# Tokens of the last feed-forward turned by VectorE and DMA instead of TensorE

## The chip, the core and the metric

The kernel runs on one core of a Trainium2 chip. A core has five engines that each work through their own queue in order: TensorE (PE in the profile, with weight loads shown apart as PEld), VectorE (DVE), ScalarE (ACT), GpSimd (POOL) and SyncE (SP, which here only issues DMAs). They wait for each other by semaphores. The metric is the device time of one execution in microseconds; the time before the change is the median of three runs.

## The reference

The input is x of 16 x 256 tokens by 256 features, float32, and the computation is a "macaron" block:

```
x = x + 0.5 * ffn(layernorm(x), w1, b1, w2, b2)
x = x + attention(layernorm(x), Wq, Wk, Wv, Wo)     # 16 heads of 16, rotary, causal
x = x + 0.5 * ffn(layernorm(x), w1, b1, w2, b2)

ffn(x) = gelu(x @ w1q.T + b1) @ w2q.T + b2          # w1q: 1024 x 256, w2q: 256 x 1024
w?q    = clip(round(w / mean(|w|)), -1, 1)          # ternary weights
```

The layernorm has no weights. Only the last of the three lines, the second feed-forward, is changed.

## The kernel before

The 4096 tokens lie in 8 blocks of 512 (NBLK = 8, TB = 512), each block as a tile xs[i] of 128 partitions by 4 token tiles by 256 features (BT = 4). `ffn(ln, after)` builds one feed-forward; ln = 0 is the first, ln = 2 the last. Its `step(u)` (line 378 on) handles u = 8 i + f: block i, chunk f of the 1024 hidden features (8 chunks of 128). A step does, in program order:

- `up(i, f)`: four matmuls (two halves of the 256 features, each with a "high" float32r part and a "rest") into a PSUM tile m of 128 x 512. ScalarE then computes gelu twice, once rounded (`h_high`) and once whole (`h_whole`), and `h_rest` = whole - high is subtracted by POOL for f = 1, 3, 5 and by VectorE for the others.
- what prepares the next blocks: statistics of block i + 2 (`stats` on VectorE, one token tile in each of f = 4 to 7, then `finish_stats`: var and rstd on POOL), the normalizing of block i + 1 into `xn` at f = 3 (`prepare`, VectorE), its transposes at f = 5 and 6 (`turn_in`: four 128 x 128 transposes on TensorE into the PSUM tile "mm", ScalarE copies them out as the high part of xnT, VectorE subtracts for the rest), and the bias b2 added to the whole of xs[i] by POOL at f = 6 (`add_bias`; at f = 1 in the last block).
- `down(i', f')` for the step two back (LATE = 2): eight matmuls, four token tiles times high and rest. After a block's last one VectorE adds half of the result to xs and `store` issues two DMAs of 256 KB on SP.

So TensorE's order is up(f), down(f - 2), up(f + 1), down(f - 1) and so on: the rest of chunk f is wanted two steps after its up projection. PSUM holds two m tiles; `h_high` and `h_rest` have five buffers, `h_whole` three, `xn` one, each part of xnT two.

The order within each engine is that of the program: vector, scalar, tensor, gpsimd and sync are wrapped so that every call keeps its place (`InOrder`, lines 164 to 176), and that is why nearly all instructions carry line 172 in the profile and are told apart by their tiles. The DMAs of `store` alone are issued through the plain queue, and the scheduler places them.

The two flat tiles that held the unquantized weights at the start (`flat1`, `flat2`, 128 x 2048) serve the attention later as work space; of flat2 it uses the first 1024 columns.

Of the kernel before, what the change touches and what calls it, by code (L numbers as in the profile page):

```python
# [8 lines left out]
FP = mybir.dt.float32  # L9
FR = mybir.dt.float32r  # L10
AF = mybir.ActivationFunctionType
# [4 lines left out]
P = 128  # L16
D = 256
KC = D // P
FF = 1024
NFC = FF // P  # L20
# [9 lines left out]
def kernel(  # L30
# [17 lines left out]
    BT = 4  # L48
    TB = BT * P
    NBLK = NT // TB  # L50
# [4 lines left out]
    fp = ctx.enter_context(tc.tile_pool(name="ffn", bufs=2))  # L55
# [19 lines left out]
    b1_sb = const.tile([P, NFC], FP, name="b1_sb")  # L75
    b2_sb = const.tile([P, D], FP, name="b2_sb")
    cos_sb = const.tile([P, 2, HD], FP, name="cos_sb")
    sin_sb = const.tile([P, 2, HD], FP, name="sin_sb")
    xs = [state.tile([P, BT, D], FP, name=f"x_{i}") for i in range(NBLK)]

    flat1, flat2 = (state.tile([P, 2 * FF], FP, name=f"w_{n}") for n in range(2))
# [19 lines left out]
    for k in range(KC):  # L101
        rows = slice(k * P, (k + 1) * P)
        nc.sync.dma_start(out=wv[:, k, :], in_=wqkvT[rows, 2 * D :])
        for at in range(0, 2 * D, 4 * HD):
            n, j, e = at // D, at // P % 2, at // (4 * HD) % 2
            nc.sync.dma_start(
                out=wqk[:, k, n, j, :, e, :],
                in_=wqkvT[rows, at : at + 4 * HD].rearrange("p (r d) -> p r d", d=HD),
            )
    for at in range(0, P, HD):  # L110
        r, n = at // 32, at // HD % 2
        nc.sync.dma_start(
            out=wo[at : at + HD, :, :],
            in_=woT.rearrange("(k n r d) f -> n r d k f", n=2, r=4, d=HD)[n, r],
# [19 lines left out]
        out=mask_k,  # L134
        in_=mask_k,
# [28 lines left out]
    class InOrder:  # L164
# [11 lines left out]
    tensor, vector, scalar, gpsimd, sync = (  # L176
        InOrder(engine) for engine in (nc.tensor, nc.vector, nc.scalar, nc.gpsimd, nc.sync)
    )
# [4 lines left out]
    def stats(ln, n):  # L183
        st = small.tile([P, 6], FP, name="st")
        vector.bn_stats(st, tokens(n))
        vector.bn_aggr(mv[ln][:, n, :], st)

    def finish_stats(ln, first, n):

        var = small.tile([P, BT], FP, name="var")  # L190
        gpsimd.tensor_scalar(
            var[:, 0:n], mv[ln][:, first : first + n, 1], LN_EPS, 1.0, ALU.add, ALU.mult
        )
        gpsimd.tensor_tensor(
            rstd[ln][:, first : first + n], var[:, 0:n], power[:, 0:n], ALU.pow
        )

    def normalize(ln, n, to, engine=None):
        (engine or vector).tensor_scalar(
            to,  # L200
            tokens(n),
            mv[ln][:, n, 0:1],
            rstd[ln][:, n : n + 1],
            ALU.subtract,
            ALU.mult,
        )
# [68 lines left out]

    LATE = 2

    def ffn(ln, after):
        xn, xnT, hT, ys = {}, {}, {}, {}

        def measure(i):
            if ln == 0:
                for t in range(BT):
                    stats(0, i * BT + t)
                finish_stats(0, i * BT, BT)

        def prepare(i, engine=None):
            xn[i] = fp.tile([P, BT, D], FP, name="xn", bufs=1)
            for t in range(BT):
                normalize(ln, i * BT + t, xn[i][:, t, :], engine)  # L290
            xnT[i] = [fp.tile([P, KC, TB], FR, name=f"xnT_{n}") for n in range(2)]

        def add_bias(i):
            gpsimd.tensor_add(xs[i], xs[i], b2_sb.unsqueeze(1).to_broadcast([P, BT, D]))

        def turn_in(i, k):
            tp = ps_mm.tile([P, TB], FP, name="mm")
            for t in range(BT):
                tensor.transpose(
                    tp[:, t * P : (t + 1) * P], xn[i][:, t, k * P : (k + 1) * P], ident  # L300
                )
            high, rest = (xnT[i][n][:, k, :] for n in range(2))
            scalar.copy(high, tp)
            return lambda: vector.tensor_sub(rest, tp, high.bitcast(FP))

        first = {}

        def up_first(i, f, to=None):
            h = first[i, f] = ps_m.tile([P, TB], FP, name="m") if to is None else to
            for n in range(2):  # L310
                for k in range(KC):
                    tensor.matmul(
                        h,
                        w1q[:, k, f * P : (f + 1) * P],
                        xnT[i][n][:, k, :],
                        start=(n == 0 and k == 0),
                        stop=(n == 1 and k == KC - 1),
                    )

        def up(i, f):  # L320
            if (i, f) not in first:
                up_first(i, f)
            h = first.pop((i, f))
            high = fp.tile([P, TB], FR, name="h_high", bufs=LATE + 3)
            rest = fp.tile([P, TB], FR, name="h_rest", bufs=LATE + 3)
            whole = fp.tile([P, TB], FP, name="h_whole", bufs=3)
            scalar.activation(high, h, AF.Gelu, bias=b1_sb[:, f : f + 1])
            scalar.activation(whole, h, AF.Gelu, bias=b1_sb[:, f : f + 1])

            engine = gpsimd if f in (1, 3, 5) and not (ln == 0 and i == NBLK - 1) else vector  # L330
            engine.tensor_sub(rest, whole, high.bitcast(FP))
            hT[i, f] = (high, rest)

        def down(i, f):
            if f == 0 and ln == 2 and i == NBLK - 1:

                ys[i] = [ps_mm.tile([P, 2, D], FP, name="mm") for t in range(0, BT, 2)]
            elif f == 0:
                y = ps_w.tile([P, BT, D], FP, name="w")
                ys[i] = [y[:, t : t + 2, :] for t in range(0, BT, 2)]  # L340
            parts = hT.pop((i, f))
            order = [(t, n) for t in range(BT) for n in range(2)]
            if ln == 2 and (i, f) == (NBLK - 1, NFC - 1):

                order = [(t, n) for n in range(2) for t in range(BT)]
            for t, n in order:

                tensor.matmul(
                    ys[i][t // 2][:, t % 2, :],
                    parts[n][:, t * P : (t + 1) * P],  # L350
                    w2q[:, f, :],
                    start=(f == 0 and n == 0 and t % 2 == 0),
                    stop=(f == NFC - 1 and n == 1 and t % 2 == 1),
                )
            if f == NFC - 1:
                for t in range(0, BT, 2):
                    xt = xs[i][:, t : t + 2, :]
                    vector.scalar_tensor_tensor(
                        xt, ys[i][t // 2], 0.5, xt, ALU.mult, ALU.add
                    )  # L360
                for t in range(0, BT, 2):
                    after(i, t)

        def begin():
            measure(0)
            if ln == 0:
                sizes(0)
            prepare(0)
            if ln == 0:
                threshold(0)  # L370
                signs(0, lambda w: w[:, :, 0 : FF // 2])
            for k in range(KC):
                turn_in(0, k)()
            if ln == 0:
                signs(0, lambda w: w[:, :, FF // 2 :])
                sizes(1)

        def step(u):
            i, f = divmod(u, NFC)
            if i < NBLK:  # L380
                up(i, f)
                if ln == 0 and u == 0:
                    threshold(1)
                if ln == 0 and u in (0, 3):
                    part = slice(0, NFC // 2) if u == 0 else slice(NFC // 2, NFC)
                    signs(1, lambda w: w[:, part, :])
                if ln == 0 and u == 4:
                    gpsimd.tensor_scalar(b2_sb, b2_sb, 0.5, 0.0, ALU.mult, ALU.add)
                if u == 1:
                    measure(1)  # L390
                if i + 1 < NBLK and (ln, i) != (2, 0):
                    if f == 3:
                        prepare(i + 1)
                    if f in (5, 6):
                        turn_in(i + 1, f - 5)()
                if f >= 4 and i + 2 < NBLK:
                    stats(ln, (i + 2) * BT + f - 4)
                    if f == NFC - 1:
                        finish_stats(ln, (i + 2) * BT, BT)
                if f == (1 if i == NBLK - 1 else 6):  # L400
                    add_bias(i)
            if u >= LATE:
                down(*divmod(u - LATE, NFC))
            if ln == 0 and u == 2 * NFC + 2:
                make_tables()
            if ln == 0 and u < (NBLK - 1) * NFC and later:
                later.pop(0)()

        return begin, step, prepare, turn_in, up_first
# [437 lines left out]
```

## Time and profile before

| What | Value |
|---|---|
| median of three runs | 602.25 us (601.55 to 603.68) |
| the profiled execution | 601.82 us, of which span 600.0 us |
| granted TensorE clock in it, mean | 0.998 |
| last feed-forward, from the first up projection of block 1 to that of block 2, and so on to block 7, by the chain | 16.03, 16.08, 16.10, 16.08, 16.10, 16.08 us |
| TensorE not busy in each of these | 0.02 us at most |
| VectorE, ScalarE, POOL busy in a block of 16.10 us | 10.55, 11.08, 7.87 us |
| DMA traffic in such a block | 34 GB/s, 0.10 of the engines' time |

The last feed-forward's steps run from about 466 us to the end. A profile line of a timeline gives the start, the duration, the engine, the line, the operation with its tiles (output <- inputs) and shapes, and in brackets how long the engine had been idle and what released it. A line of the chain gives start, duration, engine, tile and how many instructions were merged. Busy times of TensorE come from modelled ends of matmuls.

### The profile page before, as it was taken

The numbers are of one execution on the slowest core, as the hardware profiler recorded it, in microseconds if no ns is written. First come the engines' busy times: TensorE is split into PE (matmuls) and PEld (weight loads), VectorE is DVE, ScalarE is ACT, GpSimd is POOL, SyncE is SP. The second block draws the span as 40 slices with busy tenths as digits, with TensorE's granted clock in tenths as the row PEclk, the third lists the DMA queues.
The fourth block names the chain that finished last, engine by engine and source line by source line (L and its number), as shares of the span: only waits on it lengthen the run. The fifth ranks groups of instructions, "written<-read, shape, count | busy, mean of one in ns | idle before, by whom it ended". The sixth has DMA issues, their size and how long they took to land.

```text
span 600.0 us, 14402 instructions
## 1 busy us (share of the span) xinstructions
PE 581.9 (97%) x5388; PEld 467.1 (78%) x5388; DVE 475.3 (79%) x1695; ACT 391.2 (65%) x668; POOL 323.6 (54%) x297
## 2 busy tenths in 40 slices
PE   4999999999999999999999999999999999999996
PEld 3788999887777777777777777777767888888886
DVE  6877888677698998899999998888996466666643
ACT  4676766675476676676667666676665667666764
POOL 3645565693555576455765567454721354554442
PEclk9999999999999999999999999999999999999999
DMA  8810000000010001100111001100000011111101
GB/s 289 188 26 1 2 1 9 27 1 19 20 38 28 21 29 38 38 22 19 38 39 37 22 19 38 39 23 27 28 4 2 2 35 37 36 36 35 36 25 46
DMA packets 25588, 21.26 MB, mean 35 GB/s; under 512 B 11056, under 2 KB 21168, under 8 KB 25520
## 3 DMA queue, kind: packets, MB, share of 16 engines
q1 hardware_dynamic: 24960, 19.44, 10.2%
q8 instruction: 42, 0.69, 0.5%
q10 hardware_dynamic: 560, 0.92, 0.4%
q14 instruction: 26, 0.21, 0.1%
HBM read 7.51 MB, written 4.19 MB: 20 GB/s over the span
## 4 chain that ended last, share of the span: by engine, by line
PE 87%; DVE 6%; ACT 3%; issue 1%; DMA 1%; POOL 1%; DVEq 0%; SPq 0%; ACTq 0%; POOLq 0%
PE mm L172 34%; PE w L172 30%; PE m L172 23%; DVE masked L172 1%; DMA w<-in_w1T_dram 1%; DVE xn L172 1%; DVE w L172 1%; ACT h_high L172 1%; ACT h_whole L172 1%; DVE w2q L172 1%; DVE h_rest L172 1%; DVE st L172 0%; POOL h_rest L172 0%; DVE x L172 0%; ACT pT L172 0%
## 5 line engine op out<-in xcount | busy, mean ns | idle before, releaser
L172 DVE CUSTOM_DVE_ANT_0 masked<-m,mask_q 128x128 f32<-128x128 f32 x480 | 141.9, 351 | 22.2 <-PE m L172 20.9
L172 PE MATMUL m<-xnT,w1q 128*128 128x512 f32 x504 | 143.5, 406 | 0.8 <-ACT xnT L172 0.7
L172 ACT ACTIVATE pT<-w 128x768 f32<-128x768 f32 x128 | 104.1, 814 | 61.7 <-DVE w L172 61.3
L172 ACT ACTIVATE h_high<-m,b_sb 128x512 fp32r<-128x512 f32 x126 | 86.7, 688 | 79.2 <-PE m L172 79.1
L172 PE MATMUL w<-qT,kT 32*128 32x256 f32 (+1 forms) x1024 | 121.4, 348 | 1.5 <-ACT pT L172 1.5
L172 DVE TENSOR_TENSOR h_rest<-h_whole,h_high 128x512 fp32r<-128x512 f32 x83 | 74.6, 899 | 60.4 <-ACT h_whole L172 60.0
L172 PE MATMUL w<-w2q,h_high 128*128 128x256 f32 x480 | 120.7, 285 | 0.1
L172 PE MATMUL w<-w2q,h_rest 128*128 128x256 f32 x480 | 118.0, 279 | 0.7 <-POOL h_rest L172 0.7
L172 PEld LDWEIGHTS w<-qT,kT 32*128 32x128 f32 x1024 | 90.6, 184 | 35.3 <-issue 21.6
L172 PE MATMUL m<-kT,qT 32*128 32x128 f32 x960 | 116.8, 350 | 0.3 <-ACT kT L172 0.3
L172 POOL TENSOR_TENSOR h_rest<-h_whole,h_high 128x512 fp32r<-128x512 f32 x45 | 60.0, 1334 | 85.6 <-ACT h_whole L172 85.3
L172 PEld LDWEIGHTS m<-xnT,w1q 128*128 128x128 f32 x504 | 87.3, 191 | 16.3 <-DVE xnT L172 2.9
L172 PEld LDWEIGHTS w<-w2q,h_rest 128*128 128x128 f32 x480 | 90.4, 188 | 5.8 <-POOL h_rest L172 1.2
L172 PEld LDWEIGHTS w<-w2q,h_high 128*128 128x128 f32 x480 | 90.3, 188 | 5.0 <-DVE w2q L172 0.8
L172 DVE TENSOR_TENSOR w<-w,mask_k 128x512 f32<-128x512 f32 x128 | 88.9, 695 | 4.3 <-PE w L172 4.1
L172 ACT ACTIVATE h_whole<-m,b_sb 128x512 f32<-128x512 f32 x126 | 85.7, 680 | 0.0
L172 POOL TENSOR_TENSOR o<-avs,inv 128x256 f32<-128x256 f32 x32 | 20.3, 635 | 93.1 <-DVE inv L172 93.1
L172 PEld LDWEIGHTS m<-kT,qT 32*128 32x128 f32 x960 | 67.6, 185 | 2.3 <-DVE maxes L172 0.9
L172 PE MATMUL mm<-xnT_a,wqk 128*128 128x256 f32 x256 | 68.5, 392 | 0.0
L172 POOL TENSOR_TENSOR w<-w,cosT 128x512 f32<-128x512 f32 x32 | 41.2, 1288 | 26.8 <-ACT kT L172 13.5
L172 PEld LDWEIGHTS mm<-xnT_a,wqk 128*128 128x128 f32 x256 | 45.8, 189 | 10.0 <-issue 1.3
L172 POOL TENSOR_TENSOR w<-w,sinT 128x512 f32<-128x512 f32 x32 | 40.9, 1277 | 20.4 <-DMA w<-w 20.4
(86 smaller groups left out, 881.0 us busy)
## 6 DMA issues: line engine op xcount, KB each, us to landing
w<-w SPq DMA_DIRECT2D x64, 128.0 KB
out_dram<-x SPq DMA_DIRECT2D x15, 256.0 KB
x<-in_x_dram SPq DMA_DIRECT2D x7, 512.0 KB
w<-in_w2T_dram SPq DMA_DIRECT2D x1, 1024.0 KB
qT<-mT SPq DMA_DIRECT2D x64, 4.0 KB
w<-in_w1T_dram SPq DMA_DIRECT2D x1, 512.0 KB
w<-in_w1T_dram ACTq DMA_DIRECT2D x1, 512.0 KB
wqk<-in_wqkvT_dram SPq DMA_DIRECT2D x16, 32.0 KB
```

The source lines that it names most:

```text
L172: return tc.keep_in_program_order(getattr(self.engine, name)(*args, **kwargs))
```

## The change

In the last feed-forward, blocks 3 to 7 (`by_blocks`) are no longer transposed by TensorE. VectorE turns the whole normalized block in 32 x 32 pieces into the upper half of flat2 (`turned`). A DMA writes that to a DRAM tile (128 partitions of 4 KB), and four DMAs read it back in pieces of 512 bytes so that features lie on partitions, into the tile that later holds the rest part of xnT. `turn_in` then has ScalarE copy the high part from there, and VectorE subtracts in place.

The tokens come back in another order (a, n, t) than the matmuls of the down projection want, so both gelus of these blocks read and write through rearranged views with runs of 32.

For blocks 3 to 7 the work of preparing moves: statistics are taken two blocks ahead at f = 0 (one tile), 1 (one) and 2 (two), with var and rstd at f = 2; normalizing comes in two halves at f = 4 and 5 (for block 3 at f = 6 and 7), two blocks ahead; the transpose and the DMAs' issue at f = 7. In blocks 1 to 6 the bias is added in two halves at f = 2 and 3 instead of once at f = 6.

```diff
+    turned = flat2[:, FF:]
+    dram = ctx.enter_context(
+        tc.tile_pool(name="rows", bufs=2, space=bass.MemoryType.DRAM)
+    )
...
+        by_blocks = range(3, NBLK if ln == 2 else 0)
...
+        def normalize_by_blocks(i, t0, t1):
+            if t0 == 0:
+                xn[i] = fp.tile([P, BT, D], FP, name="xn", bufs=1)
+            for t in range(t0, t1):
+                normalize(ln, i * BT + t, xn[i][:, t, :])
+
+        def turn_by_blocks(i):
+            vector.transpose(turned, xn[i].rearrange("p n (j t) -> p j n t", t=32))
+            rows = dram.tile([P, 2 * TB], FP, name="rows")
+            sync.dma_start(out=rows, in_=turned)
+            of = rows.rearrange("(a f) (k j q) -> j f k a q", a=4, k=KC, j=4)
+            xnT[i] = [fp.tile([P, KC, TB], FR, name=f"xnT_{n}") for n in range(2)]
+            for j in range(4):
+                sync.dma_start(
+                    out=xnT[i][1][32 * j : 32 * j + 32]
+                    .bitcast(FP)
+                    .rearrange("p k (a q) -> p k a q", a=4),
+                    in_=of[j],
+                )
+
+        def add_bias(i, t0=0, t1=BT):
+            xt = xs[i][:, t0:t1, :]
+            gpsimd.tensor_add(xt, xt, b2_sb.unsqueeze(1).to_broadcast([P, t1 - t0, D]))
...
         def turn_in(i, k):
+            if i in by_blocks:
+                high, rest = (xnT[i][n][:, k, :] for n in range(2))
+                scalar.copy(high, rest.bitcast(FP))
+                return lambda: vector.tensor_sub(rest, rest.bitcast(FP), high.bitcast(FP))
...
-            scalar.activation(high, h, AF.Gelu, bias=b1_sb[:, f : f + 1])
-            scalar.activation(whole, h, AF.Gelu, bias=b1_sb[:, f : f + 1])
+            for to in (high, whole):
+                if i in by_blocks:
+                    to = to.rearrange("p (n a t) -> p a n t", n=BT, a=4)
+                    of = h.rearrange("p (a n t) -> p a n t", n=BT, a=4)
+                else:
+                    of = h
+                scalar.activation(to, of, AF.Gelu, bias=b1_sb[:, f : f + 1])
...
-                    if f == 3:
+                    if f == 3 and i + 1 not in by_blocks:
                         prepare(i + 1)
                     if f in (5, 6):
                         turn_in(i + 1, f - 5)()
-                if f >= 4 and i + 2 < NBLK:
-                    stats(ln, (i + 2) * BT + f - 4)
-                    if f == NFC - 1:
-                        finish_stats(ln, (i + 2) * BT, BT)
-                if f == (1 if i == NBLK - 1 else 6):
+                if i + 2 < NBLK:
+                    early = i + 2 in by_blocks
+                    for at in [(0,), (1,), (2, 3), (), (), (), (), ()][f] if early else (f - 4,):
+                        if at >= 0:
+                            stats(ln, (i + 2) * BT + at)
+                        if at == BT - 1:
+                            finish_stats(ln, (i + 2) * BT, BT)
+                    half = f - (6 if i + 2 == by_blocks.start else 4)
+                    if early and half in (0, 1):
+                        normalize_by_blocks(i + 2, 2 * half, 2 * half + 2)
+                    if early and f == 7:
+                        turn_by_blocks(i + 2)
+                if ln == 2 and 0 < i < NBLK - 1:
+                    if f in (2, 3):
+                        add_bias(i, 2 * (f - 2), 2 * (f - 1))
+                elif f == (1 if i == NBLK - 1 else 6):
                     add_bias(i)
```

More of the change, by code (lines that the diff above doesn't have):

```diff
@@ L291, in prepare @@
             xnT[i] = [fp.tile([P, KC, TB], FR, name=f"xnT_{n}") for n in range(2)]
-        def add_bias(i):
-            gpsimd.tensor_add(xs[i], xs[i], b2_sb.unsqueeze(1).to_broadcast([P, BT, D]))
+        def normalize_by_blocks(i, t0, t1):
[19 more added lines that the diff above has]
+            gpsimd.tensor_add(xt, xt, b2_sb.unsqueeze(1).to_broadcast([P, t1 - t0, D]))
         def turn_in(i, k):
+            if i in by_blocks:
+                high, rest = (xnT[i][n][:, k, :] for n in range(2))
+                scalar.copy(high, rest.bitcast(FP))
+                return lambda: vector.tensor_sub(rest, rest.bitcast(FP), high.bitcast(FP))
             tp = ps_mm.tile([P, TB], FP, name="mm")
```

## The prediction

> **What bounds the kernel now.** I read, in this order: the page's busy table and chain of waits, the chain in order of time for the last feed-forward, the timelines of GpSimd (POOL), VectorE (DVE), ScalarE (ACT) and SyncE (SP) there, and the granted clock and DMA traffic in short windows.
>
> ```profile
> span 600.0 us, 14402 instructions
> PE 581.9 (97%) x5388; PEld 467.1 (78%) x5388; DVE 475.3 (79%) x1695; ACT 391.2 (65%) x668; POOL 323.6 (54%) x297
> PE 87%; DVE 6%; ACT 3%; issue 1%; DMA 1%; POOL 1%; DVEq 0%; SPq 0%; ACTq 0%; POOLq 0%
> ```
>
> TensorE (PE) is 87% of the chain. In the part that the change touches it is all of it (chain in order of time: start, us, engine, tile):
>
> ```profile
> 508.32 0.44 PE mm L172 x4
> 508.76 0.94 PE w L172 x8
> 509.69 0.93 PE m L172 x4
> 510.62 0.44 PE mm L172 x4
> ...
> 513.87 0.69 PE m L172 x3
> 514.57 0.50 PE m L172
> ```
>
> Here "m" x4 is one up projection (0.93), "w" x8 one down projection (0.93), "mm" x4 one column half of the tokens being transposed (0.44). A step is 0.93 + 0.93 = 1.87 us and a block eight steps. Blocks start about 16.08 us apart: 8 x 1.87 = 14.9, two transposes 0.88, and about 0.26 at "514.57", where the fourth matmul of a block's first up projection is late: 0.69 + 0.50 = 1.19 instead of 0.93. The timeline shows why:
>
> ```profile
> 510.96 2.40 POOL L172 TENSOR_TENSOR x<-x,b_sb 128x1024 f32<-128x1024 f32 x1
> 511.96 1.95 DVE L172 TENSOR_TENSOR h_rest<-h_whole,h_high 128x512 fp32r<-128x512 f32 x1 [0.59 <-ACT h_whole L172]
> 513.83 0.68 DVE L172 TENSOR_TENSOR xnT<-mm,xnT 128x512 fp32r<-128x512 f32 x1
> ```
>
> The subtraction h_rest takes 0.69 elsewhere. Begun while POOL adds the bias, it ends 0.55 after POOL does (513.36 to 513.91), so the last xnT, which TensorE needs, is late. That is the first thing to carry into the change: on this chip POOL and a VectorE subtraction of two SBUF tiles exclude each other, while xnT, whose input is in PSUM, runs at 0.69 beside POOL (510.13, inside POOL's 509.70 to 510.99).
>
> The second is POOL's timing in a block:
>
> ```profile
> 485.13 1.03 POOL L172 TENSOR_TENSOR rstd<-var,power 128x4 f32<-128x4 f32 x1
> 516.28 0.19 POOL L172 TENSOR_SCALAR var<-mv 128x4 f32<-128x4 f32 x1 [2.92 <-DVE mv L172]
> 517.71 1.10 PE L172 MATMUL m<-xnT,w1q 128*128 128x512 f32 x4
> 519.59 1.09 PE L172 MATMUL m<-xnT,w1q 128*128 128x512 f32 x4
> 520.15 0.69 DVE L172 TENSOR_TENSOR h_rest<-h_whole,h_high 128x512 fp32r<-128x512 f32 x1 [0.88 <-ACT h_whole L172]
> 522.06 1.29 POOL L172 TENSOR_TENSOR h_rest<-h_whole,h_high 128x512 fp32r<-128x512 f32 x1 [2.44 <-ACT h_whole L172]
> 471.22 0.39 PE L172 MATMUL w<-w2q,h_rest 128*128 128x256 f32 x1 [0.34 <-POOL h_rest L172]
> ```
>
> The up projections of f = 2 and 3 start at 517.71 and 519.59; their rests can start 2.44 (DVE) and 2.47 (POOL) later. POOL sat idle 2.44 us before the rest of f = 3. The last line is an instance of TensorE waiting for a late POOL rest.
>
> **Removed.** Five blocks (3 to 7) lose two transposes each: 10 x 0.44 = 4.4 us off TensorE's chain. Nothing else can take that room, so it is gained whole unless a wait fills it.
>
> **Bias in halves at f = 2 and 3 (blocks 1 to 6).** The full addition leaves f = 6, so the last rests and xnT no longer meet it: six stalls of 0.26 = 1.6. VectorE now does the normalizing and the xnT subtraction from SBUF in that place, both of which can wait for POOL; I keep 1.4 as gained. Bounds: 0 to 1.6.
>
> **What stands on POOL's queue.** This is the step that I think decides. In the built kernel's order POOL runs in blocks 1 to 5: rest f = 1, var, rstd, first bias half, rest f = 3, second half, rest f = 5. Var waits for the statistics of the block two ahead, now done at f = 0, 1 and twice at f = 2 on VectorE, the last two behind the rest of f = 2. Times from the start of the up projection of f = 2:
> - VectorE's rest starts at 2.44; the next operation starts 0.61 later; two pairs of statistics take 0.55 + 0.64 (st 0.42, aggregate 0.18, gaps). Done at 4.24.
> - POOL: var starts 0.09 later, 4.33; rstd 0.27 after that, 4.60, and takes 1.03: 5.63.
> - First bias half, 128x512: the page's POOL products of that shape take 1288 ns: 6.92.
> - The rest of f = 4 on VectorE is ready at 2 x 1.87 + 2.44 = 6.18, held by the bias half, so it goes first when that ends: 0.55, to 7.47.
> - Rest of f = 3 on POOL, ready since 1.87 + 2.47 = 4.34: 7.47 + 1.30 = 8.77; if it goes before VectorE's, 8.22.
> - TensorE wants it for the second matmul of the down projection of f = 3, after up f = 5: 3 x 1.87 + 0.93 + 0.12 = 6.65.
>
> So TensorE waits 1.6 to 2.2 us per block, counting up to 0.1 from release to matmul. I take 2.15, the case in which VectorE's waiting rest goes first, as in the row at 513.36. In block 1 the transposes of block 2 still stand before that matmul (0.44 more cover): 1.8. Together 4 x 2.15 + 1.8 = 10.4; bounds 5 x 1.6 - 0.4 = 7.6 and 5 x 2.25 = 11.3. Block 6 has the halves but no statistics: its first half ends before the rest of f = 3 is ready, no cost. After the stall POOL runs the second half and rest f = 5, ending about 11.5; TensorE asks for that at 12.6, so it is covered by 1.1.
>
> **VectorE's transpose, 128x1024.** Rows: 128x256 from SBUF 437 ns, 128x512 from PSUM 717. Their slope gives 1.28, four times the first 1.75. It stands between the rest of f = 7 and that of f = 0, which it just reaches: 1.28 costs nothing, 1.75 up to 0.5 once or twice and later statistics. I take 0, range 0 to 2.5. Against it stands the Trainium skill, VectorE: DVE Perf Modes, "Rules for kernel authors": for a full 128x128 transpose use TensorE. By that rule alone the 4.4 would not be a gain; the chain rows decide that it is.
>
> **DMAs.** SP's built order is: rows to DRAM, two stores of the block before, four reads. The reads stand behind stores that wait for the down projection of f = 7. Counted from a block's start: the transpose ends near 2.5, the rows' DMA needs about 2.9 (a pair of 256 KB stores issued at 518.70 had moved its data by 521.3, at 340 GB/s, and some 0.3 for completion); the stores go out at about 5.0 and 5.7, the reads (0.4 to 0.55 each to issue) from 6.0 to 8.0. Store traffic ends near 7.6; 512 KB of reads at 340 GB/s end near 9.5, at a third of that rate near 12.5. ScalarE copies from them at 11.7 at the earliest and, with the stall above, may do so until 14.5. (The stores' issue, and two of the short windows, whose last three columns are granted clock, DMA share and GB/s:)
>
> ```profile
> 518.70 0.97 SPq L743 DMA_DIRECT2D out_dram<-x  x2
> 520.10:520.50 0.40, 0.40 (x3) 0.33 (x2) 0.35 (x1) 0.01 (x1) 0.00 (x0) 1.00 1.04 353
> 598.25:598.50 0.25, 0.00 (x0) 0.00 (x0) 0.00 (x0) 0.00 (x0) 0.00 (x0) 0.50 0.99 332
> ```
>
> So I charge 0. Bounds 0 and, at the 50 GB/s that 64-byte pieces got near 24 us, 10 us of reading, some 3.3 late per block: 15. The pieces here are 512 bytes, nearer to the loads' 1 KB at 350 GB/s. The stores, queued behind the rows' wait for the transpose, have no reader; the last block's, which end the kernel, have no rows before them.
>
> **Gelu writing in pieces of 32.** The vals copy writes pieces of 16 at 372 ns, as long as the contiguous mT copy: 0, upper bound 0.04 each, 0.4 in all. The xnT subtraction now reads SBUF twice and waits for POOL's rest of f = 5; it ends near 12.0 and 13.9 after the base above, TensorE wants the second at 14.1, so no cost. The Trainium skill, SBUF — State Buffer, "Who interferes with whom", says that a VectorE instruction with two SBUF inputs contends with POOL's reads. If each waited a whole POOL rest and this were on the path, an estimate by that page would add 5 x 1.3.
>
> **Sum.** -4.4 - 1.4 + 10.4 = +4.6. The profiled run took 601.82 (span 600.0, 1.82 around it): 606.4. The median of the runs shown is 602.25, 0.43 above it: 606.9. Ends of the main case: -6.0 + 7.6 = +1.6 and -4.4 - 0.5 + 11.3 = +6.4, plus transposes +2.5: 603.9 to 611.
>
> **Rivals.**
> - POOL in time: the wait at down f = 3 isn't there, and the gains stand: 602.25 - 5.8 = 596.4. It needs var, rstd and the half to end by 5.3 instead of 6.92; below a stall of 1.16 per block (5.8 / 5) the change is faster. For it: POOL is busy only 54%. Against: it is a queue in order, and each duration is a row. 0.11.
> - Reads late: they land after 14.5, that is at less than some 75 GB/s. Then ScalarE, with gelu queued behind the copy, holds the block's first up projection: up to 602.25 + 4.6 + 15 = 622. 0.06.
> - VectorE the bound: a slower transpose and normalizing held by POOL make it late at two more places; 1 us in each of 5 blocks: 612. Or TensorE's clock falls in the stalls: it was still 1.00 until 598.0, 2.5 us after the last matmul (near 595.5), and 0.50 from 598.25; stalls of over 2.6 might halve it. 0.06.
> - Main 0.75; gain and loss cancel, 0.02.
>
> **Range and chances.** 603.2 to 611.5 holds the main case and part of the third rival. Faster by over 0.3% (about what a measurement of this kernel can tell from none) 0.11, within it 0.04, slower 0.85.
>
> **What would show it.** Right: down f = 3 with an idle of about 2 us released by POOL's h_rest, five times; var about 2 us before it; no "mm" transposes in blocks 3 to 7; blocks 2 to 5 about 17.1 us apart, the last ones 15.0. Wrong: POOL's rest of f = 3 ending within 0.8 of its old place, or TensorE waiting for the xnT copy, that is for DMA.

## The result and the profile after

The changed kernel takes 607.93 us (median of six runs, 606.12 to 608.31) against 602.45 us for the kernel before (now the median of six runs, 601.55 to 603.68): a ratio of 1.0084, 95% interval 1.0072 to 1.0095, so it is slower by 5.5 us. The forecast was 606.9. The profiled execution has a span of 605.2 us, 5.2 more than before.

The page after, its span, busy times and the chain's shares by engine:

```profile
span 605.2 us, 14447 instructions
PE 577.6 (95%) x5348; PEld 463.8 (77%) x5348; DVE 489.8 (81%) x1700; ACT 391.4 (65%) x668; POOL 324.8 (54%) x303
PE 77%; DVE 8%; POOL 5%; ACT 4%; issue 3%; DMA 2%; SPq 0%; DVEq 0%; POOLq 0%; ACTq 0%
```

TensorE has 40 matmuls and 4.3 us of busy time less, as it should have without ten transposes of four matmuls each. But its share of the chain has fallen from 87% to 77%, and POOL and VectorE have come in. The chain in order of time shows one of the places, in block 3 (start, us, engine, tile; st holds statistics):

```profile
521.20 0.95 PE m L172 x4
522.17 0.69 ACT h_high L172
522.86 0.58 ACT h_whole L172
...
523.53 0.69 DVE h_rest L172
524.23 0.35 DVE st L172
...
525.40 0.19 POOL var L172
...
525.68 0.11 POOL rstd L172
525.79 0.88 issue
526.67 1.29 POOL x L172
527.96 1.69 POOL h_rest L172
529.65 0.04 issue
529.70 1.09 PE w L172 x7
```

The up projection of f = 2, its gelu, VectorE's rest of f = 2, the statistics behind it, then on POOL var, rstd ("issue" is the rest of its 1.02 us), the first half of the bias, the rest of f = 3, and only then TensorE's down projection. That is the queue that the forecast had written out. The list of waits from 480 us on gives it its size. "A <- B" says that A waited for B, and the columns are total us, times, the longest:

```profile
PEld w L172 <- POOL h_rest L172: 10.3, 5, 2.2
PE w L172 <- POOL h_rest L172: 8.8, 5, 1.9
```

These are five waits, one in each of blocks 1 to 5, seen once at the weight load and once at the matmul. No other wait of TensorE's in that stretch is over 0.3 us. The timelines of POOL, VectorE and TensorE at the same place show each step (start, us, engine, operation; in brackets idle before and releaser):

```profile
525.68 1.02 POOL L172 TENSOR_TENSOR rstd<-var,power 128x4 f32<-128x4 f32 x1
526.67 1.29 POOL L172 TENSOR_TENSOR x<-x,b_sb 128x512 f32<-128x512 f32 x1
527.91 1.73 POOL L172 TENSOR_TENSOR h_rest<-h_whole,h_high 128x512 fp32r<-128x512 f32 x1
...
527.20 1.32 DVE L172 TENSOR_TENSOR h_rest<-h_whole,h_high 128x512 fp32r<-128x512 f32 x1 [1.89 <-ACT h_whole L172]
...
527.57 0.28 PE L172 MATMUL w<-w2q,h_high 128*128 128x256 f32 x1
529.70 0.39 PE L172 MATMUL w<-w2q,h_rest 128*128 128x256 f32 x1 [1.85 <-POOL h_rest L172]
```

VectorE's rest of f = 4 is held by the bias half (1.32 instead of 0.69), then holds POOL's rest of f = 3 (1.73 instead of 1.30). TensorE's second matmul of the down projection would have followed at 527.69, 0.12 after the first, and comes at 529.70, 2.0 us late.

By the chain the blocks 1 to 6 are now 17.73, 17.04, 17.07, 17.05, 17.05 and 14.94 us apart; they were 16.03 to 16.10. Here are the first up projections of blocks 2 and 3, and of blocks 6 and 7:

```profile
500.42 0.93 PE m L172 x4
...
517.46 0.93 PE m L172 x4
...
568.63 0.93 PE m L172 x4
...
583.57 0.93 PE m L172 x4
```

The last feed-forward is taken from the start of ScalarE's load of the gelu table to that of VectorE's last addition. These lines bound it, two of the kernel before and two of the changed one:

```profile
466.09 1.28 ACT L172 ACT_TABLE_LOAD   x1
595.41 1.29 DVE L172 SCALAR_TENSOR_TENSOR x<-mm,x 128x512 f32<-128x512 f32 x2 [0.66 <-PE mm L172]
...
467.02 1.28 ACT L172 ACT_TABLE_LOAD   x1
600.48 1.29 DVE L172 SCALAR_TENSOR_TENSOR x<-mm,x 128x512 f32<-128x512 f32 x2 [0.67 <-PE mm L172]
```

It was 595.41 - 466.09 = 129.32 and is 600.48 - 467.02 = 133.46: 4.14 longer. Of the rest of the 5.2 in the span, 0.93 us lies ahead of it, among instructions that are the same in both programs, and 0.1 behind it. In the nine profiled executions of this study that table load starts anywhere from 465.98 to 467.88, while the table load before it starts within 165.85 to 166.40, so most of this difference arises between the two. Why is not settled here, so the experiments are read by both measures.

The clock bears on the 5.5 between the medians as well. Four of the six runs of the changed kernel had a mean granted TensorE clock of 0.996 or 0.997, and took 607.90 to 608.31 us. The other two had 0.998 and 0.999, and took 606.12 and 606.99; the slower of these is the profiled one. In the 63 runs of the experiments' rounds, which include runs of the kernel before, the mean was never under 0.998. In the nine traces the clock is under 1.00 only after the last matmul, which leaves a mean of 0.998 or more. So in those four runs the clock seems to have fallen at another place too. Where, and whether TensorE's waits brought it about, is not shown, as none of these four left a trace. The other two runs alone are 4.1 slower than the kernel before (606.55 - 602.45), as much as the feed-forward is longer.

### The profile page after: what moved, and what is told of

Its sections match the earlier page's. It is cut to its first block, busy times and chain, and to the rows that moved or that the text cites. A ratio compares the mean times of both kernels' runs of the same rounds, so it can differ in the third digit from the quotient of the medians.

```text
span 605.2 us, 14447 instructions
## 1 busy us (share of the span) xinstructions
PE 577.6 (95%) x5348; PEld 463.8 (77%) x5348; DVE 489.8 (81%) x1700; ACT 391.4 (65%) x668; POOL 324.8 (54%) x303
## 4 chain that ended last, share of the span: by engine, by line
PE 77%; DVE 8%; POOL 5%; ACT 4%; issue 3%; DMA 2%; SPq 0%; DVEq 0%; POOLq 0%; ACTq 0%
PE mm L172 30%; PE w L172 26%; PE m L172 20%; POOL h_rest L172 2%; POOL w L172 1%; DVE masked L172 1%; ACT h_high L172 1%; DVE h_rest L172 1%; ACT h_whole L172 1%; POOL x L172 1%; DMA w<-w 1%; DVE st L172 1%; DMA w<-in_w1T_dram 1%; DVE w L172 1%; DVE xn L172 1%
## 5 line engine op out<-in xcount | busy, mean ns | idle before, releaser
L172 PE MATMUL m<-xnT,w1q 128*128 128x512 f32 x504 | 141.6, 404 | 0.7 <-ACT xnT L172 0.7
L172 DVE TENSOR_TENSOR h_rest<-h_whole,h_high 128x512 fp32r<-128x512 f32 x83 | 71.3, 859 | 59.7 <-ACT h_whole L172 59.2
L172 POOL TENSOR_TENSOR h_rest<-h_whole,h_high 128x512 fp32r<-128x512 f32 x45 | 62.3, 1385 | 90.9 <-ACT h_whole L172 90.7
```

Source lines behind the costliest of these rows:

```text
L172: return tc.keep_in_program_order(getattr(self.engine, name)(*args, **kwargs))
```

## The experiments

The theory was that POOL's queue decides: the rest of f = 3 stands behind var, which waits for statistics, and behind rstd and a bias half. Its rivals were that VectorE and POOL exclude each other whatever the order, that VectorE is too full, that the split bias alone is at fault, and that tokens come late from DRAM.

| Kernel | Median us | Last feed-forward us | Against 129.32 |
|---|---|---|---|
| changed kernel | 607.93 | 133.46 | +4.14 |
| var and rstd behind the rest of f = 3 | 598.18 | 125.11 | -4.21 |
| rest of f = 3 on VectorE | 601.78 | 128.46 | -0.86 |
| bias whole at f = 6 | 607.45 | 133.80 | +4.48 |
| early statistics | 597.33 | 124.07 | -5.25 |
| bias halves alone | 601.07 | 127.63 | -1.69 |
| early statistics, reads ahead of stores | 597.65 | 123.38 | -5.94 |
| early statistics, turned a step later | 599.38 | 125.10 | -4.22 |

**Var and rstd behind the rest of f = 3.**

```diff
-                        if at == BT - 1:
+                        if at == BT - 1 and not early:
                             finish_stats(ln, (i + 2) * BT, BT)
+                    if early and f == 3:
+                        finish_stats(ln, (i + 2) * BT, BT)
```

> One move against the changed kernel: in blocks 1 to 5 var and rstd are issued behind POOL's rest of f = 3 instead of ahead of it. Queue theory (the rest of f = 3 is late because it stands behind work that waits for statistics): TensorE's wait at the down projection of f = 3, 2.0 us five times, goes; rstd now comes some 4 us later, so VectorE normalizes later and the xnT subtraction costs about 0.7 at the first up projection of blocks 3 to 6. Worked out: 602.45 - 4.4 - 1.4 + 4 x 0.7 = 599.4, range 597 to 601. Rival, exclusion of VectorE and POOL (they hold each other up whatever the order on POOL): the same work collides, 606 or more. Rival, TensorE waits for the tokens from DRAM: no change, 608.

Measured: 598.18 us, ratio to before 0.9923 (0.9907 to 0.9938). Two small instructions, moved behind the two larger ones that follow them in POOL's queue, turn a loss of 5.5 us into a gain of 4. From block 1 on, TensorE's waits no longer name POOL, and the wait that is left is for xnT. The chain shows the new order, and VectorE's line how long normalizing takes there:

```profile
PE m L172 <- DVE xnT L172: 0.8, 4, 0.2
PEld m L172 <- DVE xnT L172: 2.5, 4, 0.6
...
505.62 1.29 POOL h_rest L172
...
506.99 0.19 POOL var L172
...
507.27 1.03 POOL rstd L172
...
508.32 0.77 DVE xn L172
...
508.32 2.69 DVE L172 TENSOR_SCALAR xn<-x,mv,rstd 128x256 f32<-128x256 f32 x2 [0.19 <-POOL rstd L172]
```

What is left is the other wait that I expected here, xnT at the first up projections. Normalizing now starts behind the later rstd and runs while POOL is busy (2.69 us for two), so the xnT behind it is late. Blocks are 15.39 us apart there, 0.45 over 14.94, and I had taken 0.7. Exclusion as such, and the DRAM trip, fall as causes of the loss: both are still in this kernel. So does the half by itself, which still stands ahead of the rest of f = 3; what delays it is the pair that waits for statistics.

**The rest of f = 3 on VectorE.**

```diff
-            engine = gpsimd if f in (1, 3, 5) and not (ln == 0 and i == NBLK - 1) else vector
+            on_pool = (1, 5) if ln == 2 and i + 2 in by_blocks else (1, 3, 5)
+            engine = gpsimd if f in on_pool and not (ln == 0 and i == NBLK - 1) else vector
```

> In blocks 1 to 5 the rest of f = 3 is subtracted by VectorE instead of POOL, all else as in the changed kernel. Queue theory: the wait at the down projection of f = 3 goes, but POOL's rest of f = 5 still stands behind rstd and both bias halves and VectorE has 0.69 more: about 0.7 at the down projection of f = 5 and 0.9 at the next first up projection, in four blocks. 602.45 - 5.8 + 4 x 1.6 = 603, range 600 to 605. Rival, VectorE is the engine that is too full (489.8 us busy): one more subtraction on it makes it slower than 608.

Measured: 601.78 us, ratio 0.9991 (0.9980 to 1.0002). TensorE's waits of some size:

```profile
PE m L172 <- DVE xnT L172: 3.2, 4, 0.8
PEld w L172 <- POOL h_rest L172: 1.0, 4, 0.3
```

The big wait goes although VectorE has one subtraction more per block, so VectorE's fullness is not the cause. The new waits cost 1.28 us a block (blocks 16.22 apart) where I expected 1.6, and eat most of the gain.

**The bias left whole at f = 6.**

```diff
-                if ln == 2 and 0 < i < NBLK - 1:
-                    if f in (2, 3):
-                        add_bias(i, 2 * (f - 2), 2 * (f - 1))
-                elif f == (1 if i == NBLK - 1 else 6):
+                if f == (1 if i == NBLK - 1 else 6):
                     add_bias(i)
```

> The tokens turned as in the changed kernel, but the bias left whole at f = 6 as before. Queue theory: without the first half ahead of it the rest of f = 3 starts after rstd, 5.6 us after the up projection of f = 2, and ends 0.3 to 0.4 late, so that wait shrinks from 2.0 to 0.4; the whole bias of 2.4 us then meets the normalizing and xnT, which now read SBUF twice, and costs about 1.9 at the first up projection of blocks 3 to 7. 602.45 - 4.4 + 5 x 0.4 + 4 x 1.9 = 607.6, range 604 to 610: slow as before, but with the wait in another place. Rival, only the split bias is at fault: 598.

Measured: 607.45 us, ratio 1.0079 (1.0062 to 1.0097). The same loss, in another place:

```profile
PE m L172 <- DVE xnT L172: 7.2, 5, 1.5
PEld w L172 <- POOL h_rest L172: 2.0, 4, 0.7
```

Without the half in front, the rest of f = 3 is late by little; but the whole addition of 2.4 us now holds VectorE's normalizing and xnT. So the bias had to move once the tokens are turned from SBUF; it was moved into a place that was also taken.

**Early statistics.** Statistics two each at f = 0 and 1, var and rstd at f = 2, bias halves at f = 1 and 3, normalizing at f = 5 and 6.

```diff
-                    for at in [(0,), (1,), (2, 3), (), (), (), (), ()][f] if early else (f - 4,):
+                    for at in [(0, 1), (2, 3), (), (), (), (), (), ()][f] if early else (f - 4,):
...
-                        if at == BT - 1:
+                        if at == BT - 1 and not early:
                             finish_stats(ln, (i + 2) * BT, BT)
-                    half = f - (6 if i + 2 == by_blocks.start else 4)
+                    if early and f == 2:
+                        finish_stats(ln, (i + 2) * BT, BT)
+                    half = f - (6 if i + 2 == by_blocks.start else 5)
...
-                    if f in (2, 3):
-                        add_bias(i, 2 * (f - 2), 2 * (f - 1))
+                    if f in (1, 3):
+                        add_bias(i, f - 1, f + 1)
```

> All of the change kept, its pieces placed so that POOL never has a rest behind something that waits: statistics two each at f = 0 and 1, var and rstd at f = 2, bias halves at f = 1 and 3, normalizing at f = 5 and 6. Queue theory: POOL is through with rstd by the time that the rest of f = 3 is ready; nothing is left at the down projection of f = 3 and at most 0.1 at the first up projections: 602.45 - 4.4 - 1.4 = 596.7, range 595.8 to 598.5, faster than both kernels. Rival, exclusion of VectorE and POOL: as much work of both in the same block, 604 or more. Rival, reads from DRAM barely in time: they are asked for 2 us earlier against the block's work when the wait is gone, so TensorE waits for the xnT copy instead, 600 or more.

Measured: 597.33 us, ratio 0.9908 (0.9886 to 0.9930): faster than both kernels. From block 1 on, TensorE has no wait for POOL left. One wait of some size and of another kind shows, in one block, in ScalarE's and SP's timelines (its reads, and those of the round after it for comparison):

```profile
535.66 3.67 SPq L172 DMA_DIRECT2D xnT<-rows  x4
...
541.94 0.62 ACT L172 CAST xnT<-xnT 128x512 fp32r<-128x512 f32 x1 [1.26 <-DMA xnT<-rows]
...
551.33 2.54 SPq L172 DMA_DIRECT2D xnT<-rows  x4
```

ScalarE waits 1.26 us for the reads, and block 5's first up projection is 0.7 late. The feed-forward is 5.25 shorter; all of the ten transposes (10 x 0.44 = 4.4) and the six small stalls (6 x 0.26 = 1.56) would be 5.96.

**The bias halves alone.**

```diff
-        by_blocks = range(3, NBLK if ln == 2 else 0)
+        by_blocks = range(NBLK, NBLK)
```

> The bias halves of the change alone: TensorE transposes all blocks as before, statistics, normalizing and var/rstd at their old places. Theory: the six stalls of 0.26 at the first up projections go, since nothing of POOL's meets the last rests there; in block 1 the second half may hold VectorE's normalizing at f = 3. 602.4 - 1.6 + 0.5 = 601.3, range 600.6 to 602. Rival, the halves themselves delay POOL's rest of f = 3: 603 or more. Rival, the 0.26 comes from something else: 602.4.

Measured: 601.07 us against 602.78 in the same rounds, ratio 0.9970 (0.9958 to 0.9982). The six stalls of 0.26 are gone: no block's first up projection shows a late fourth matmul, block 2's for instance reads

```profile
498.77 0.93 PE m L172 x4
```

The feed-forward is 1.69 shorter, and the 0.5 that I added for block 1 doesn't appear. So the 0.26 was POOL's bias holding VectorE, and this half of the change gains by itself: POOL's queue has nothing waiting in it at f = 2.

**Reads ahead of stores.** On top of the early statistics, the stores' DMAs keep their program order.

```diff
-        parts = [(t, 2, nc.sync)]
+        parts = [(t, 2, sync)]
         if (i, t) == (NBLK - 1, BT - 2):
-            parts = [(t, 1, nc.sync), (t + 1, 1, nc.scalar)]
+            parts = [(t, 1, sync), (t + 1, 1, scalar)]
```

> The version with early statistics, and the stores of the output kept in program order, so that the four reads from DRAM are issued on SP as soon as the rows have landed and not behind a store that waits for the down projection. In that version ScalarE waited 1.26 us for the reads of one block and 0.36 in another, and TensorE lost 0.7 there. Theory: reads go out about 0.9 us sooner and no 256 KB store runs beside them; those waits go: 597.3 - 0.7 = 596.6, range 595.8 to 597.5. Rival, the reads' own traffic is slow in that block and not their start: the wait stays, 597.3.

Measured: 597.65 us, ratio 0.9910 (0.9897 to 0.9924); by medians it is not told apart from the version before it. In its one profile the wait is gone, and the feed-forward is 0.69 shorter, 5.94 in all, which is the whole of 5.96:

```profile
534.98 3.17 SPq L172 DMA_DIRECT2D xnT<-rows  x4
...
540.97 0.62 ACT L172 CAST xnT<-xnT 128x512 fp32r<-128x512 f32 x1
```

**Turned a step later.** On top of the early statistics, the transpose and its DMAs go from f = 7 to f = 0 of the next block.

```diff
+                if f == 0 and i + 1 in by_blocks:
+                    turn_by_blocks(i + 1)
...
-                    if early and f == 7:
-                        turn_by_blocks(i + 2)
```

> The version with early statistics, and VectorE's transpose with its DMAs issued one step later (f = 0 of the next block instead of f = 7), to measure how much cover the trip through DRAM has. In that version the first copy of a block waited 0 to 1.26 us for the reads. Theory: the rows land 1.9 us later and with them the reads 1.3 to 1.9, of which TensorE absorbs about 0.5: 5 blocks x 0.8 to 1.4 = 4 to 7, so 602.5, range 599.5 to 605, with TensorE waiting for xnT at the first up projections. Rival, the trip has 2 us and more of cover in most blocks, as I worked out beforehand: 597 to 598.5.

Measured: 599.38 us, ratio 0.9938 (0.9921 to 0.9954), feed-forward 1.0 longer than with early statistics: a miss between the two stated cases. In the first round the reads were issued only 0.7 later (rows at 503.53, reads at 506.70; with early statistics alone 502.23 and 506.00), and ScalarE waits for them in all five rounds, of which three:

```profile
511.76 0.62 ACT L172 CAST xnT<-xnT 128x512 fp32r<-128x512 f32 x1 [0.80 <-DMA xnT<-rows]
...
526.99 0.62 ACT L172 CAST xnT<-xnT 128x512 fp32r<-128x512 f32 x1 [0.84 <-DMA xnT<-rows]
...
542.89 0.62 ACT L172 CAST xnT<-xnT 128x512 fp32r<-128x512 f32 x1 [1.51 <-DMA xnT<-rows]
```

4.4 us of waiting on ScalarE cost TensorE 1.7, taken against the version in which ScalarE never waits for reads (125.10 - 123.38): some 0.5 of each wait is absorbed. So with POOL's wait gone the DRAM trip, begun a step later, has no cover to spare at ScalarE, and about half a microsecond more at TensorE. I had carried the whole delay of 1.3 to 1.9 over to ScalarE and most of it to TensorE; both were too much.

## Why the prediction was right

- **What POOL's queue would cost.** Counted from the up projection of f = 2 (521.04 in the timeline), forecast and measured: VectorE's rest starts 2.44 and 2.49; var 4.33 and 4.36; rstd 4.60 and 4.64; first half 5.63 and 5.63; its end 6.92 and 6.92; VectorE's rest of f = 4 ends 7.47 and 7.48; rest of f = 3 ends 8.77 and 8.60. The order "VectorE's waiting rest goes first" was the one that occurred. Only the last step is off by more than 0.05: POOL's rest took 1.73 from 527.91 on, partly beside VectorE's, where I had counted 1.30 after it. A block's wait is 17.05 - 14.94 = 2.11 for the 2.15 taken, block 1's 17.73 - 16.03 = 1.7 for 1.8: 10.1 in all (4 x 2.11 + 1.7) for 10.4. The experiments with var and rstd moved, and with the rest moved to VectorE, show that it is the place in this queue.
- **Transposes, 4.4.** Right, and whole: with the waits out of the way the feed-forward is 5.94 shorter, 4.4 of it from here.
- **The small stalls, 1.4.** They were worth all of 1.56; the halves alone gave 1.69.
- **Transpose on VectorE, 0.** It took 1.24 (1.28 by the slope) and cost nothing; its line is below. The Trainium skill (VectorE: DVE Perf Modes, "Rules for kernel authors") would leave a 128x128 transpose to TensorE where the result may go to PSUM. Here, where TensorE is the bound and VectorE's 32 x 32 pieces are put in place by DMAs, the measurement goes the other way as soon as nothing waits.
- **Gelu in pieces of 32, 0.** 690 and 681 ns for 689 and 680.
- **xnT from SBUF, 0.** It does wait for POOL, 1.19 on average for 0.68, as the Trainium skill says of two SBUF inputs (SBUF — State Buffer, "Who interferes with whom"). The normalizing, with one SBUF tile, waits for POOL too. Here both stood beside TensorE's longer wait and cost nothing. With var and rstd moved, where that wait is gone but the normalizing comes later, xnT cost 0.45 a block; with early statistics that cost is gone.
- **DMAs, 0.** Right for this kernel, with less room than I wrote. The reads ran at about 180 GB/s and not 340, and four issues took 2.56 us and not 2. Their traffic ended near 527.5, 10.2 after the block's start (517.3), between my 9.5 and 12.5; ScalarE copied at 528.92, 11.6 after it, and didn't wait. With early statistics ScalarE got them 5.1 us after their first issue in one round (506.00 to 511.11) and 6.3 in the slow one (535.66 to 541.94).
- **Sum.** 10.1 - 4.4 - 1.56 = 4.14, which is the measured 4.14 of the feed-forward, for a forecast of 4.6. The remaining distance to the medians' 5.5 stayed open: 0.93 of the profiled execution lies ahead of the feed-forward, and four of the six runs have a lower mean clock. A clock that falls in the stalls was part of a rival that I gave 0.06; the profiled execution, at 1.00 in its waits, doesn't show it, and the other runs neither show it nor rule it out.
- **Upper end of the range.** It takes 0.5 off for the small stalls where my own lower bound for them was 0; the sum would end 0.5 higher, near 611.6. The result lies far inside either way.

The lines behind the middle points, from block 3 (VectorE's transpose and an xnT that waits for POOL, then the reads' issue and ScalarE's copy):

```profile
518.47 1.24 DVE L172 STREAM_TRANSPOSE w<-xn 128x1024 f32<-128x1024 f32 x1
531.01 1.78 DVE L172 TENSOR_TENSOR xnT<-xnT,xnT 128x512 fp32r<-128x512 f32 x1
...
523.18 2.56 SPq L172 DMA_DIRECT2D xnT<-rows  x4
...
528.92 0.62 ACT L172 CAST xnT<-xnT 128x512 fp32r<-128x512 f32 x1
```

## What to carry to other kernels

An engine that is busy 54% of the time can still set the end. When a step is moved to "where there is room", write out the queue of its engine at that place, instruction by instruction, with what each waits for: a few small ones that wait for another engine delay everything behind them. And when the same work can be placed so that nothing waits at the head of a queue, do that before the idea is given up: here it was worth some 10 us, from +5.5 to -5.

## What the runs showed of the hardware that was not expected

The four reads of 128 KB in 512-byte pieces took SP 0.61 us each to issue (median in the changed kernel), where a store of 256 KB took 0.38. In the round of block 3 they moved at 174 to 226 GB/s, where stores moved at about 340. The DMA engines were busy 0.58 to 0.76 of the time then, and 128 KB in 0.61 us is 215 GB/s, so the issue may be what set the rate; that is not shown. In every kernel that had them, the third round of reads took longer to issue (3.30 in the changed kernel, 3.67 with early statistics, 3.15 to 3.52 in others, against 2.54 to 2.68); why is not known. In the profiled execution TensorE's clock stayed at 1.00 through waits of 2 us, as these windows show (us, busy times and counts of TensorE, its weight loads, VectorE, ScalarE and POOL, then clock, DMA share, GB/s):

```profile
526.00:526.50 0.50, 0.50 (x6) 0.50 (x6) 0.00 (x0) 0.50 (x2) 0.50 (x1) 1.00 0.58 176
...
528.50:529.00 0.50, 0.00 (x0) 0.00 (x0) 0.50 (x2) 0.50 (x2) 0.50 (x1) 1.00 0.00 0
```

VectorE's normalizing, one SBUF tile and two columns, is held by POOL as the subtraction is: two took 2.65 us while POOL ran the rest of f = 3 and the second half, and 0.72 once POOL was idle:

```profile
528.44 2.65 DVE L172 TENSOR_SCALAR xn<-x,mv,rstd 128x256 f32<-128x256 f32 x2
...
532.72 0.72 DVE L172 TENSOR_SCALAR xn<-x,mv,rstd 128x256 f32<-128x256 f32 x2
```
